# Two moves in a graph-attention kernel: the second batch's channel means ahead of the last query products of the first, and the last batch's first pair normalised a few steps later

## Chip, cores and metric

The kernel runs on one core of a Trainium2 chip. The core has five engines with a queue of instructions each: TensorE (PE; its weight loads are listed as PEld), VectorE (DVE), ScalarE (ACT), GpSimd (POOL) and SyncE (SP), which here issues the DMAs. The metric is the time of one execution in microseconds, as the median over several. Before the change it is 2466.79 us over 8 runs (2463.55 to 2468.76).

## Reference, cut to what matters

Two layers over `x` (16 batches of 1024 rows with 256 channels), both with the 1024x1024 matrix `adj`:

```python
def layer0(x, A):                      # graph convolution, batch norms
    A_norm = A + eye(n)
    deg = sum(A_norm, axis=0) + sum(A_norm, axis=1) - diagonal(A_norm)
    A_hat = A_norm * rsqrt(deg)[:, None] * rsqrt(deg)[None, :]
    agg = einsum('nm,bmd->bnd', A_hat, x)
    h = relu(batchnorm(agg @ W1.T + b1))
    return batchnorm(h @ W2.T + b2)

def layer1(x, para, adj, kv_w):        # gated graph, attention of 4 heads
    fea = transpose(x, (0, 2, 1))
    c_adj = mean(fea, axis=1)          # channel mean of each row
    diff = c_adj[:, None, :] - c_adj[:, :, None]
    A = abs(abs(sigmoid(diff) - 0.5) - 0.5) * 2.0
    Wg = adj * (A + transpose(A)) * 0.5
    q = relu(einsum('bcn,bnm->bcm', fea, Wg) * para)
    k, v = x @ kv_w
    return softmax(q k^T * scale) v    # per head

x = layernorm(x + layer0(x, adj))
x = layernorm(x + layer1(x, para, adj, kv_w))
```

All in fp32.

## The kernel before

The program orders its instructions itself: each engine's queue is filled in the order in which the Python code issues them, and no scheduler moves them. Waits follow from data and from buffers.

Layer 0 fills the first third of the time. Layer 1 runs over the 16 batches. A batch has 16 *steps*; a step `g` takes two blocks of 128 keys, one pair of heads and half of the queries. `scores(g)` (L787, tile `s`) makes the products of keys and queries into PSUM, `exps(g)` (L799, ScalarE) the exponentials `e`, `sums(g)` (L805, L808, VectorE) adds them up into `acc`, and `attend(g)` (L823, PE) multiplies them with the values into `o`. The tiles `s` have two buffers, which one step fills: the scores of step g+1 wait for the exponentials of step g. At the end of a pair of heads, `attend` copies one half of `o` on ScalarE (L834) and adds the other on VectorE (L835), as `ot`. `dens` (L852, tile `pd`) sums `acc` over the keys by PE once both pairs are done.

Around the steps lies the work for other batches, in pieces that are put into slots: 8 slots for each batch, two for each turn of the main loop, which covers four steps. A turn issues the pieces of its two slots first (sorted by `arrange`), then, for each of its steps k, the scores and exponentials of k+1 and the sums and products of k. A dictionary `between` holds pieces that are issued behind step k instead.

The pieces that matter here:

- `ln1_b` (L646, ScalarE) ends the first layer norm, and accumulates each row's sum in `cs`.
- `means` (L679, L681, VectorE) scales `cs` to the channel means and makes half of them (`hcs`).
- `crow` makes one row of 1024 means, the same on every partition. For batch 0 it does that on PE (L692). For the others it transposes `cs` on PE (L696, tile `pc`), copies 8x128 numbers on ScalarE (L698), writes them to DRAM (L699) and reads them back broadcast to 128 partitions (L700). The tile `crow` has one buffer.
- `gate`: `wg_a` makes a gate tile on ScalarE from `crow` and `hcs` or `cs` (L710, or L712 and L713), `wg_b` finishes it on VectorE with `adj` (L719, L720) and loads the next `adj` tile. Batch 1's gates belong to the first steps of batch 0's attention.
- `keys` (L736, tile `pk`, copied on ScalarE in L739), `values` (L747, tile `pv`, copied in L754), `graph` and `queries` (L769, L770).
- `x1_t` (L675, L676) transposes the normed rows on PE and copies them on VectorE, tile `px`.
- `finish_a` joins a pair of row blocks of the output and takes their moments on VectorE, with `rs` and `nm` on GpSimd (L66, L68, L914); `finish_b` normalises the pair on ScalarE (L922, two instructions) and stores it (L925). `back` (tile `pf`) and `recips` (tile `pr`, L868) serve the last half batch.

Before the first step stands an opening: eight turns of `opening`, in which batch 0's gate products (`graph0`, L1098) are accumulated over k = 0 to 7 and batch 1's rows are prepared by the lists in `second_rows`. With the last product the four query tiles are made on VectorE, out of the PSUM buffers that the first scores then take. `means(1)` follows the pieces of k = 7, and `crow(1)` is put into `between[-1]`, behind the scores and exponentials of step 0.

In the last batch (`b == B - 1`) the slots t_a and t_b of `finish_a` and `finish_b` for the first half of the queries (`hf = 0`) are worked out by the branch `elif not by_pe(b, hf)`: for the first pair (k = 0) slots 4 and 6, for the second 6 and 9. So `finish_b(15, 0)` is issued ahead of step 252's turn, in front of the exponentials of step 253.

Of the kernel before, what the change touches and what calls it, by code (L numbers as in the profile page):

```python
# [22 lines left out]
def gnn_norm_attention_kernel(  # L23
# [17 lines left out]
    B, N, C = x.shape  # L41
# [529 lines left out]
    def fast():  # L571
      with ExitStack() as fx:
# [105 lines left out]
        def means(b):  # L678
            nc.vector.tensor_scalar_mul(css[b], css[b], 1.0 / C)  # L679
            hcs[b] = sm.tile([P, NT], F32, tag="hcs", bufs=2, name=f"hcs_{b}")  # L680
            nc.vector.tensor_scalar_mul(hcs[b], css[b], 0.5)  # L681
# [130 lines left out]
        def by_pe(b, hf):  # L812
            return b == B - 1 and hf == NH - 1
# [143 lines left out]
        NC = NS // 2  # L957
        NK = NT // 2
        at, between = {}, {}

        def put(w, t, f, *a):
            at.setdefault(w * NC + t, []).append((f, a))
# [4 lines left out]
        for b in range(B):  # L967

            for hf in range(NH):
                t = (hf + 1) * (NC // NH)  # L970
                put(b, t, dens, b, hf)
                if by_pe(b, hf):
                    put(b, t, recips, b, hf)
                for k in range(KB // 2):
                    j = hf * (KB // 2) + k

                    if b * NH + hf < B * NH - 3:
                        t_f, t_a, t_b = (t + 1, t + 2 + k, t + 6 + k) if hf == 0 else (t + 1, t + 4 + k, t + 6 + k)
                    elif not by_pe(b, hf):

                        t_f, t_a, t_b = t, t + 2 * k, t + 2 + 2 * k if b < B - 1 else (t + 2, NC + 1)[k]
                    else:
                        t_f, t_a, t_b = t, t + 1 + k, t + 2 + k
                    put(b, t_f, back if by_pe(b, hf) else fetch_o, b, j)
                    if t_a == t:
                        between[(b * NC + t) * 2 + NK // 2] = [(finish_a, (b, j))]
                    else:
                        put(b, t_a, finish_a, b, j)
                    put(b, t_b, finish_b, b, j)
            if b == 0:  # L990
                continue

            if b > 1:
                put(b - 2, 2, begin, b)
                for j in range(NT // 2):
                    put(b - 2, j, load, b, j)
                    put(b - 2, j + 1, bn2_q, b, j)
                    put(b - 2, j + 2, rows, b, j)
                    put(b - 2, j + 2, ln1_a, b, j)
                    put(b - 2, j + 3, ln1_b, b, j)  # L1000
                    put(b - 2, j + 3, put_x1, b, j)
                    put(b - 2, 5 + j // 2 * 2, get_x1, b, j)
                    put(b - 2, min(6 + j, NC), x1_v, b, j)
                put(b - 2, NC - 2, means, b)
                put(b - 2, NC - 1, crow, b)

            i = 0
            for t, n in enumerate(WG):
                for i in range(i, i + n):
                    put(b - 1, t, gate, b, i)  # L1010
                i += 1
            kv = [(keys, (b, c, h)) for h in range(NH) for c in range(CT)]
            kv += [(values, (b, j)) for j in range(0, NT, 2)]
            for t, n in enumerate(KV):
                for _ in range(n):
                    f, a = kv.pop(0)
                    put(b - 1, t, f, *a)
            m = 0
            for t, n in enumerate(QG):
                for m in range(m, m + n):  # L1020
                    put(b - 1, NC - len(QG) + t, graph, b, m)
                m += 1
# [64 lines left out]
        def gate0(i):  # L1087
            wg_a(0, i)
            wg_b(0, i)
# [3 lines left out]
        def graph0(k):  # L1093
            if k == 0:
                PG0.extend(ps_s.tile([P, 2, FB], F32, tag="s", name=f"pg0_{h}") for h in range(NH))
            for h in range(NH):
                for c in range(CT):
                    nc.tensor.matmul(  # L1098
                        PG0[h][:, c, :],
                        x1s[0, k // 2][:, k % 2, ts(c, P)],  # L1100
                        wgs[0, k][:, ts(h, FB)],
                        start=(k == 0),
                        stop=(k == NT - 1),
                    )
            if k == NT - 1:
                for h in range(NH):
                    for c in range(CT):
                        queries(0, c, h, PG0[h][:, c, :])
# [27 lines left out]
        for c in range(CT):  # L1136
# [18 lines left out]
            3: [(rows, 2), (ln1_a, 2), (ln1_b, 1)],  # L1155
            4: [(x1_t, 0), (rows, 3), (ln1_a, 3)],
            5: [(ln1_b, 2), (x1_t, 1)],
            6: [(ln1_b, 3), (x1_t, 2)],
            7: [(x1_t, 3)],
        }  # L1160

        def opening(s):

            k = s + NC
            if 0 <= k < NC:
                for i in range(3 + 2 * k, min(5 + 2 * k, NT)):
                    gate0(i)
                graph0(k)
                for f, j in second_rows[k]:
                    f(1, j)  # L1170
                if k == NC - 1:
                    means(1)
                    between[-1] = [(crow, (1,))]

        for t in range(-NC // 2, max(max(at) // 2, nsteps // NK - 1) + 1):
            g = NK * t
            now = [p for s in (2 * t, 2 * t + 1) for p in [(opening, (s,))] + arrange(at.get(s, []))]
            behind = max((k + 1 for k, fa in enumerate(now) if is_short(fa)), default=0)  # L1180
            for k in range(len(now) + 1):
                if k == behind and 0 <= g < nsteps:
                    sums(g)
                if k < len(now):
                    f, a = now[k]
                    f(*a)
            for k in range(g, g + NK):
                if 0 <= k + 1 < nsteps:
                    scores(k + 1)
                    exps(k + 1)  # L1190
                if 0 <= k < nsteps:
                    if k > g:
                        sums(k)
                    attend(k)
                for f, a in between.pop(k, ()):
                    f(*a)
# [6 lines left out]
        )  # L1203

    flag = fast()


# [155 lines left out]
```

## Time and profile before

| what | value |
|---|---|
| median of 8 runs | 2466.79 us (2463.55 to 2468.76) |
| the profiled execution: time | 2468.01 us |
| the profiled execution: span from first to last instruction | 2466.2 us |
| mean granted clock of TensorE | 0.992 |
| ScalarE's exponentials (L799): 512, each | 1020 ns |
| VectorE's sums of exponentials (L808): 384, each | 1329 ns |
| ScalarE's first gates (L710): 80, each (median) | 1152 ns |
| ScalarE's normalising (L646): 128, each | 594 ns |

Lines of the order of time show: start and duration in us, engine, line, operation, output and inputs, shape, how many were merged, and in brackets how long the engine sat idle before and what ended that. Lines of waits show: engine and line that waited, for whom, total us, times, the longest. The granted clock is the share of full speed that TensorE's clock was let through at. The chain of waits from the last instruction back is no help here: the page follows it no further than the last normalisation (L922), so the places are read from the order of time.

### The profile page before, as it was taken

The page shows a single profiled execution, that of the slowest core. Times are in us where ns is not written, and L with a number is a line of the kernel's source. Part 1 is how long each engine was busy: PE and PEld are TensorE (multiplying, and loading weights), DVE is VectorE, ACT ScalarE, POOL GpSimd, SP SyncE. Part 2 cuts the span into 40 slices and gives each one's busy share as a digit, 9 for nine tenths or more (in the row PEclk, how much of TensorE's full clock was granted, in tenths as well). Part 3 has the DMA queues.
Part 4 walks back from the last instruction along what each step waited for, and adds up shares of the span by engine and source line. Part 5 has one row for each costly group of instructions (what it writes and reads, how often), then busy time and mean ns, then how long its engine had stood idle before and what let it go on. Part 6 is the DMA issues. An engine that isn't in the chain of part 4 may idle for free. (4 is left out here: it accounts for less than half of the span.)

```text
span 2466.2 us, 33875 instructions
## 1 busy us (share of the span) xinstructions
PE 2415.9 (98%) x12217; PEld 1009.8 (41%) x12217; DVE 1812.4 (73%) x2583; ACT 1094.5 (44%) x1549; POOL 777.2 (32%) x826
## 2 busy tenths in 40 slices
PE   8999999999999899999999999999999999999997
PEld 4444444444444433443434434344343343443432
DVE  5545545555776767888788888888888888888676
ACT  2000000002554455664655646656566565564644
POOL 2222232321556421314223233232332322414012
PEclk9999999999999899999999999999999999999998
DMA  3122122222677543545545545545354454554221
GB/s 137 68 86 103 71 85 101 94 77 85 213 268 265 133 120 73 149 110 121 144 101 133 140 97 146 122 118 145 82 151 114 118 148 95 139 127 109 68 44 50
DMA packets 583951, 292.73 MB, mean 119 GB/s; under 512 B 407528, under 2 KB 556512, under 8 KB 576608
## 3 DMA queue, kind: packets, MB, share of 16 engines
q1 hardware_dynamic: 583776, 290.49, 43.1%
q8 instruction: 98, 1.61, 0.3%
q14 instruction: 77, 0.63, 0.1%
HBM read 194.46 MB, written 95.94 MB: 118 GB/s over the span
## 5 line engine op out<-in xcount | busy, mean ns | idle before, releaser
L799 ACT ACTIVATE e<-s 128x1024 f32<-128x1024 f32 x512 | 496.1, 1020 | 332.1 <-PE s L787 270.6
L808 DVE TENSOR_TENSOR acc<-acc,e 128x1024 f32<-128x1024 f32 x384 | 510.2, 1329 | 115.3 <-ACT e L799 88.9
L787 PE MATMUL s<-qT,kT 64*64 64x512 f32 x4096 | 493.8, 597 | 10.9 <-ACT e L799 8.3
L823 PE MATMUL o<-e,v 64*64 64x512 f32 x4096 | 487.0, 590 | 0.0
L761 PE MATMUL pg<-wg,x 128*128 128x512 f32 x960 | 426.5, 597 | 0.0
L614 POOL TENSOR_TENSOR yt<-yt,stq 128x512 f32<-128x512 f32 x120 | 182.2, 1519 | 414.4 <-DMA yt<-yT 252.0
L761 PEld LDWEIGHTS pg<-wg,x 128*128 128x128 f32 x960 | 178.7, 190 | 238.6 <-issue 237.8
L823 PEld LDWEIGHTS o<-e,v 64*64 64x64 f32 x4096 | 157.3, 134 | 285.4 <-issue 277.7
L787 PEld LDWEIGHTS s<-qT,kT 64*64 64x64 f32 x4096 | 147.6, 133 | 306.3 <-issue 254.0
L107 ACT COPY u<-pa 128x512 f32<-128x512 f32 x15 | 8.8, 586 | 475.3 <-PE pa L312 475.3
L66 POOL TENSOR_SCALAR rs_z<-mv_z 128x2 f32<-128x2 f32 x64 | 18.2, 285 | 474.6 <-DVE mv_z L563 453.7
L720 DVE SCALAR_TENSOR_TENSOR wg<-wg,adj 128x1024 f32<-128x1024 f32 x128 | 162.8, 1303 | 2.8
L312 PE MATMUL pa<-AhT,x 128*128 128x512 f32 x360 | 161.8, 592 | 0.0
L646 ACT ACTIVATE x<-x,nm_a,rs_a 128x256 f32<-128x256 f32 x128 | 75.9, 594 | 171.9 <-POOL nm_a L636 171.5
L835 DVE TENSOR_TENSOR ot<-o,ot 128x512 f32<-128x512 f32 x64 | 44.3, 692 | 130.8 <-ACT ot L834 130.8
L747 PE MATMUL pv<-kvw,x1T 128*128 128x256 f32 x512 | 118.7, 385 | 1.3 <-ACT kT L739 1.3
L736 PE MATMUL pk<-x1T,kvw 128*128 128x512 f32 x256 | 117.8, 604 | 0.0
L66 POOL TENSOR_SCALAR rs_a<-mv_a 128x2 f32<-128x2 f32 x64 | 38.0, 593 | 237.8 <-DVE mv_a L563 236.6
L343 PE MATMUL ph<-agg,SW 128*128 128x512 f32 x240 | 112.8, 592 | 0.0
L747 PEld LDWEIGHTS pv<-kvw,x1T 128*128 128x128 f32 x512 | 96.9, 192 | 33.4 <-issue 16.0
L312 PE MATMUL pa<-T,sx 128*128 128x512 f32 x240 | 107.9, 592 | 0.0
L312 PEld LDWEIGHTS pa<-AhT,x 128*128 128x128 f32 x360 | 68.4, 190 | 86.1 <-issue 86.1
(193 smaller groups left out, 3148.7 us busy)
## 6 DMA issues: line engine op xcount, KB each, us to landing
adj<-in_adj_dram SPq DMA_DIRECT2D x128, 512.0 KB
h<-hT SPq DMA_DIRECT2D x28, 1024.0 KB
hL<-h SPq DMA_DIRECT2D x28, 1024.0 KB
ob<-o SPq DMA_DIRECT2D x248, 72.0 KB
x<-in_x_dram SPq DMA_DIRECT2D x16, 1024.0 KB
yT<-y SPq DMA_DIRECT2D x64, 256.0 KB
out_dram<-r SPq DMA_DIRECT2D x64, 256.0 KB
xr<-in_x_dram SPq DMA_DIRECT2D x62, 256.0 KB
```

The costliest lines, as they stand in the source:

```text
L312: nc.tensor.matmul(p, xs[n][:, k, :], bs[n][:, k, :], start=(k == 0), stop=(k == KN - 1))
L343: nc.tensor.matmul(p, ws[n][:, ts(f, P)], bs[n], start=True, stop=True)
L614: nc.gpsimd.tensor_tensor(y, y, sc, op)
L646: nc.scalar.activation(r, r, AF.Identity, bias=nm[:, a : a + 1], scale=rs[:, a : a + 1], accum_out=css[b][:, i : i + 1])
L720: nc.vector.scalar_tensor_tensor(t, t, 1.0, adjs[b * NT + i], op0=OP.add, op1=OP.mult)
L736: nc.tensor.matmul(p, kvw[:, k, ts(c, P)], x1Ts[b][:, k, ts(h, FB)], start=(k == 0), stop=(k == CT - 1))
L747: nc.tensor.matmul(p[:, ts(a, C)], x1Ts[b][:, k, ts(j + a, P)], kvw[:, k, C:], start=(k == 0), stop=(k == CT - 1),)
L761: nc.tensor.matmul(pg[b], x1s[b, k // 2][:, k % 2, ts(c, P)], wgs[b, k][:, ts(h, FB)], start=(k == 0), stop=(k == NT - 1))
L787: nc.tensor.matmul(t[r * HD : (r + 1) * HD, h, :], kTs[b, pair][h * HD : (h + 1) * HD, ts(2 * cb + r, HD)], qTs[b, pair, hf][h * HD : (h + ...
L799: nc.scalar.activation(E[g, a], S.pop((g, a)), AF.Exp)
L808: nc.vector.tensor_add(ACC[b, hf, pair], ACC[b, hf, pair], E[g, a])
L823: nc.tensor.matmul(O[b, hf, pair][r][h * HD : (h + 1) * HD, :], vs[b][r * HD : (r + 1) * HD, cb, pair * P + h * HD : pair * P + (h + 1) * HD],
```

## The change

Two edits, in the lists that set the order.

In the opening, `means(1)` and `crow(1)` are issued with k = 6: the means behind `ln1_b(1, 3)`, the row behind the transposes of the third pair, so ahead of the products of k = 7, batch 0's queries and the first scores. `second_rows` takes None for a piece that has no pair.

In the last batch, `finish_b(15, 0)` leaves slot 6 and goes into `between`, behind step 254, so behind the exponentials of steps 253, 254 and 255.

```diff
@@ -979,6 +979,9 @@
                         t_f, t_a, t_b = t, t + 2 * k, t + 2 + 2 * k if b < B - 1 else (t + 2, NC + 1)[k]
+                        if b == B - 1 and k == 0:
+                            between[(b * NC + t_b) * 2 + NK // 2] = [(finish_b, (b, j))]
+                            t_b = None
                     else:
                         t_f, t_a, t_b = t, t + 1 + k, t + 2 + k
@@ -986,7 +989,8 @@
                     else:
                         put(b, t_a, finish_a, b, j)
-                    put(b, t_b, finish_b, b, j)
+                    if t_b is not None:
+                        put(b, t_b, finish_b, b, j)
@@ -1155,7 +1159,7 @@
-            6: [(ln1_b, 3), (x1_t, 2)],
+            6: [(ln1_b, 3), (means, None), (x1_t, 2), (crow, None)],
             7: [(x1_t, 3)],
@@ -1167,10 +1171,7 @@
                 for f, j in second_rows[k]:
-                    f(1, j)
-                if k == NC - 1:
-                    means(1)
-                    between[-1] = [(crow, (1,))]
+                    f(1) if j is None else f(1, j)
```

The lines behind the edits move by one (L1098 of before is L1102 after); the number of instructions stays.

## The prediction

> **What bounds the kernel now.** I read the page's busy shares first, then TensorE's waits over the span, then the order of time around each place that the change touches, and the granted clock there.
>
> ```profile
> span 2466.2 us, 33875 instructions
> PE 2415.9 (98%) x12217; PEld 1009.8 (41%) x12217; DVE 1812.4 (73%) x2583; ACT 1094.5 (44%) x1549; POOL 777.2 (32%) x826
> ...
> PE s L787 <- ACT e L799: 8.3, 3, 3.5
> ...
> PE pv L747 <- ACT kT L739: 1.3, 1, 1.3
> ```
>
> TensorE (PE) is busy for 98% of the span, so a change gains only where PE waits. Attention's score products (`s`) wait for ScalarE's exponentials (`e`) three times, 8.3 us in all. Two of the three lie where the change works: 3.13 us in the opening of the attention, 3.46 us in the last batch.
>
> The opening, in order of time (start, duration, engine, line; idle before it and its releaser in brackets):
>
> ```profile
> 866.11 0.69 DVE L676 COPY x1T<-px 128x512 f32<-128x512 f32 x1 [3.18 <-PE px L675]
> ...
> 872.98 0.27 PE L696 MATMUL pc<-ident,cs 128*8 128x128 f32 x1
> 873.09 7.03 PE L736 MATMUL pk<-x1T,kvw 128*128 128x512 f32 x16
> 873.83 0.24 ACT L698 COPY crow<-pc 8x128 f32<-8x128 f32 x1
> 874.09 0.35 SPq L699 DMA_DIRECT2D crow_d<-crow  x1
> 875.32 0.34 SPq L700 DMA_DIRECT2D crow<-crow_d  x1
> 879.74 1.15 ACT L710 ACTIVATE wg<-crow,hcs 128x1024 f32<-128x1024 f32 x1 [5.67 <-DMA crow<-crow_d]
> 881.41 1.99 PE L747 MATMUL pv<-kvw,x1T 128*128 128x256 f32 x8 [1.29 <-ACT kT L739]
> 889.49 1.92 ACT L799 ACTIVATE e<-s 128x1024 f32<-128x1024 f32 x2
> 890.55 3.36 PE L787 MATMUL s<-qT,kT 64*64 64x512 f32 x16 [3.13 <-ACT e L799]
> 895.73 1.90 PE L787 MATMUL s<-qT,kT 64*64 64x512 f32 x16
> ```
>
> The row of channel means (`crow`) goes out through DRAM and back: 874.07 (copy's end) to 879.74, 5.67 us. ScalarE sits in front of its first gate activation until then. Its queue then holds 9.75 us of gates and copies (879.74 to 889.49) ahead of the exponentials that PE needs. PE pays 1.29 us before `pv`, and 3.13 us before `s`.
>
> The last batch, and the granted clock there (in the last two lines the columns are stretch, length, busy time of PE, PEld, DVE, ACT and POOL with counts, then the clock):
>
> ```profile
> 2433.25 1.90 PE L823 MATMUL o<-e,v 64*64 64x512 f32 x16
> 2436.56 1.09 ACT L922 ACTIVATE r<-r,nm,rs_z 128x256 f32<-128x256 f32 x2 [4.22 <-POOL nm L914]
> 2438.61 3.69 PE L787 MATMUL s<-qT,kT 64*64 64x512 f32 x16 [3.46 <-ACT e L799]
> 2439.97 5.21 DVE L808 TENSOR_TENSOR acc<-acc,e 128x1024 f32<-128x1024 f32 x4
> 2450.01 1.07 PE L852 MATMUL pd<-acc,ones 128*32 128x512 f32 x8
> 2452.94 0.26 DVE L868 RECIPROCAL RD<-pr 128x16 f32<-128x16 f32 x1 [1.51 <-PE pr L866]
> ...
> 891.00:892.00 1.00, 1.00 (x11) 0.23 (x7) 1.00 (x1) 0.41 (x1) 0.97 (x1) 0.50 0.98 348
> 2440.00:2441.00 1.00, 1.00 (x8) 0.25 (x4) 1.00 (x2) 0.34 (x1) 0.79 (x1) 0.50 0.00 0
> ```
>
> ScalarE waits 4.22 us for GpSimd's `nm` with the exponentials queued behind. After both long waits of PE the granted clock is 0.50: `s` takes 3.36 and 3.69 us for 16 where other rows have 1.90. From stretch to stretch the clock is low from about 890.9 to 894.4 and from 2437.2 to 2444.0.
>
> **Part 1, the means earlier.** Moved: two VectorE scalings (L679, L681; 0.16 and 0.17 us), one PE transpose, one ScalarE copy (0.24 us), two DMAs. As built, VectorE does the scalings ahead of the L676 copy at 866.11. Their input, ScalarE's last row sum, ends at 864.38, and VectorE is idle for 3.18 us there: cost nothing; without that idle time, 0.33 us on the way to the queries. The copy behind the scalings would wait if the sums came late.
>
> PE does the transpose after the third `px` group, at about 865.9. Its input is then over 1 us old. It takes 0.11 us of PE (872.98 to 873.09), taken back at 872.98. Its PSUM buffer and that of the last `px` group change places; both were long free. `crow` has one buffer, whose last reader of batch 0 starts at 847.59 and takes 1.1 us. SyncE's queue: the last load ahead was issued by 853.30, so nothing holds the DMAs; batch 2's first loads, behind them, go up to 7.5 us earlier too, into DMA engines with a share of 0.00 from 860 to 872. GpSimd is passed by nothing.
>
> So the copy starts at about 866.3, ends at 866.55, and with the same 5.67 us the row is back at 872.2. ScalarE gets free only after its second exponential, 1.02 us from 872.91+0.11 = 873.02, at 874.05. The row is 1.8 us early, and the gates start at 874.05 instead of 879.74.
>
> From there I step both queues forward with the durations of before. `pk` runs 872.95 to 879.85 without a wait for `kT`; ScalarE now waits a little for `pk`. `pv` to 881.7; `s` to 883.45; `o` to 885.2. ScalarE: the fourth `kT` copy from 879.98, a gate from 880.5, `v` from 881.87 (it needs `pv`), two activations to 884.5, first exponential to 885.5. PE waits 0.3 us for it instead of 3.13 us, too little to lower the clock by any row here. `s` then begins at 885.55, loses 0.1 us on the second exponential, `o` from 887.4, and the `s` of 895.73 comes at 889.1: **6.6 us**. Bounds: 7.1 us if ScalarE never held PE (`s`, `o`, `s`, `o` from 881.7 end at 888.6, at the 1.72 us from start to start that undisturbed groups show), 5.0 us where the clock had stayed full in the kernel before (5.18 us from 890.55 to 895.73 would have been about 3.5). I take 6.6, the stepping through this profile. Between 895.73 and 2400 PE waits nowhere for ScalarE or a DMA, so the shift stays to the end.
>
> **Part 2, the first finished pair later.** Two ScalarE activations (1.09 us) and a store move behind the last exponentials. No other DMA is passed on SyncE's queue, nothing on GpSimd's. In times of before, the exponential after L834's copy starts at 2432.6, its two parts end by 2434.6, and PE goes from `o` (2433.25) straight on: `s` 2434.97, `o` 2436.7, `s` 2438.4, two `o` groups to 2443.55. Before they ended at about 2450.0. The moved activations run from 2441.4 to 2442.5, ahead of the last L834 copy at 2443.6, so they are hidden; without that gap they would cost up to 1.09 us.
>
> But VectorE doesn't move. From 2428.47, where it gets `ob` by DMA, it works without a gap until 2439.97, and the six sums L808 follow, 7.8 us by the six at 2407.19 (7.87), to 2447.8. `pd`, the sums over keys, needs them. Before, they ended at 2449.53 and PE's `o` set the time. At full clock: half of `pd` from 2447.93, eight `pf` transposes (0.117 us apart) after `ot` at 2448.5, four `pr`, reciprocal at 2450.1: 2.8 us before 2452.94. But PE then has stood for 3.8 to 4.3 us, longer than both waits after which the clock was 0.50. At half clock `pd` takes 1.0 instead of 0.5, `pf` 1.9 instead of 0.94, `pr` 1.1 instead of 0.6: reciprocal at 2451.9, **1.1 us** gained. I take this end, the nearest rows being the 3.13 and 3.46 us waits; 2.8 stays as a bound, and 0 below, where the kernel before had kept its clock (then its `o` would have ended at 2447.3, with VectorE in charge).
>
> The Trainium skill, page "TensorE: Matmul & The Clock Gate", section "What's actually happening", says that the clock is halved after an idle window of about 3.4 us, and that the windows run freely and don't start with the work. It speaks against part 2, which makes a longer gap than it closes. The stretches agree: 890.9 to 894.4 is one such window, 2437.2 to 2444.0 two. By it a gap of 3.8 us that falls across two windows could leave the clock full, and part 2 would give 2.8 us; by the rows alone it gives 1.1 us.
>
> **The sum.** 6.6 + 1.1 = 7.7 us. The profiled execution took 2468.01 us, 1.8 us beyond its span; 2460.3 after the change. It is 1.2 us above the median of 2466.79, so I predict 2459.1 us.
>
> **Rivals.**
> 1. The tail keeps its clock: 6.6 + 2.8 = 9.4 us, 2457.4. For it: half of `pd` can run before the gap. Against: both gaps of this size here were followed by 0.50.
> 2. The kernel before mostly pays less for its clock than the profile shows: 5.0 + 0, 2461.8. For it: the profiled execution is above the median by 1.2 us. Against: 1.2 us is less than the 2.7 us that it would take.
> 3. The row comes back late, and ScalarE's wait stays in part. At 3 us later than 874.05 part 1 gives 3.6 us, 2462.1 with part 2; at 5.7 us later nothing, 2465.7. Against: idle DMA engines, 1.8 us to spare. This is also where the change would not do what it says.
> 4. Slower: the transpose now stands in PE's queue ahead of the last query products. If the last row sum were late, PE would stand there. GpSimd feeds it, and its three steps took 0.22, 0.71 and 0.50 us; in other rows the same take 1.02, 1.74 and 4.58. With the slow ones the scalings end at about 870.6, PE stands 4.7 us and runs up to two low stretches (3.4 us lost). That eats 8.1 of 7.7: 2467.2, and more with later sums. It begins from sums 1.2 us late and passes the gain from about 5.5 us. Against: VectorE's work beside GpSimd there is the same as before.
>
> **How the numbers follow.** Forecast 0.62, rival 1 0.13, rival 2 0.12, rival 3 0.10, rival 4 0.03. The range 2456.0 to 2463.5 takes rivals 1, 2 and most of 3, with about 1.3 us for the spread of the median (single runs lie within 2463.55 to 2468.76). 0.2% is 4.9 us, about what a measurement of this kernel can tell from no change: under 2461.9 is faster. Forecast, rival 1 and half of rival 2 lie there: 0.81. Slower by as much needs more than rival 4's price: 0.02. The rest, 0.17, is the same.
>
> **What would show it.** Right: `pc` ahead of the last query products, the gates from about 874 with no DMA wait, no wait of 1 us of PE from 873 to 890, clock 1.00 there; in the last batch no wait of ScalarE for `nm` before the exponentials, no wait of `s`, instead `pd` waiting some 4 us for VectorE's `acc`, at clock 0.50. Wrong: a wait for `crow`, a wait of PE for `cs` near 866, or the 6.6 us given back before 2400.

## Result, and the profile after

| | median us | runs |
|---|---|---|
| before | 2466.68 | 32 |
| changed | 2460.16 (2458.43 to 2462.45) | 12 |

The ratio is 0.9974, with a 95% interval of 0.9966 to 0.9981: 6.5 us less, where 7.7 us were forecast (2459.1; the range was 2456.0 to 2463.5). The profiled execution of the changed kernel took 2460.43 us, 7.6 us less than the profiled one of before.

TensorE is busy for 2412.5 us of a span of 2458.7, 98% as before. Two lines from the list of its waits in the changed kernel (engine and line that waited, for whom, total us, times, longest):

```profile
PE pd L852 <- DVE acc L808: 2.7, 1, 2.7
...
PE s L787 <- ACT e L799: 1.7, 1, 1.7
```

Of the three waits of the scores for the exponentials (8.3 us) only the one of 1.7 us that the change doesn't touch is left. A longer one is new: `pd`, the sums over keys, waits for VectorE.

The opening of the changed kernel, in order of time (PE, ScalarE, SyncE put together by start):

```profile
866.04 0.60 PE L675 MATMUL px<-ident,x 128*128 128x128 f32 x4
866.47 0.27 PE L696 MATMUL pc<-ident,cs 128*8 128x128 f32 x1
866.78 0.25 ACT L698 COPY crow<-pc 8x128 f32<-8x128 f32 x1 [1.83 <-PE pc L696]
868.29 0.34 SPq L700 DMA_DIRECT2D crow<-crow_d  x1
874.51 1.14 ACT L710 ACTIVATE wg<-crow,hcs 128x1024 f32<-128x1024 f32 x1
886.03 2.00 PE L787 MATMUL s<-qT,kT 64*64 64x512 f32 x16
889.57 1.90 PE L787 MATMUL s<-qT,kT 64*64 64x512 f32 x16
```

The gates (L710) begin at 874.51 straight behind the second exponential, with no bracket: nobody waits for the row any more. The scores of 886.03 have no bracket either; before they sat idle for 3.13 us. To compare executions I count from the third `px` group, since layer 0 ended 0.57 us later in this one (866.04 against 865.47): to the scores of 889.57 it takes 23.53 us, where before it took 30.26 us (865.47 to 895.73). The opening gave 6.73 us. This counts a stretch at half clock that the profile of before had in its opening (890.9 to 894.4) and this one has not; it is worth some 1.7 us (5.18 us from 890.55 to 895.73, where two undisturbed groups take 3.44).

The last batch of the changed kernel, in order of time, and then one stretch of its granted clock (stretch, length, busy time and count of PE, PEld, DVE, ACT, POOL, clock, DMA share, GB/s):

```profile
2427.02 1.90 PE L823 MATMUL o<-e,v 64*64 64x512 f32 x16
2428.73 1.90 PE L787 MATMUL s<-qT,kT 64*64 64x512 f32 x16
...
2433.26 7.87 DVE L808 TENSOR_TENSOR acc<-acc,e 128x1024 f32<-128x1024 f32 x6
2437.43 1.05 PE L852 MATMUL pd<-acc,ones 128*32 128x512 f32 x4
2441.18 1.80 PE L852 MATMUL pd<-acc,ones 128*32 128x512 f32 x4 [2.70 <-DVE acc L808]
2444.67 0.65 PE L866 MATMUL pr<-ident,dt 128*128 128x128 f32 x4
```

```profile
2442.00:2443.00 1.00, 1.00 (x5) 0.09 (x2) 0.00 (x0) 0.00 (x0) 0.00 (x0) 0.50 0.00 0
```

The scores run on behind `o` without a gap. VectorE's six sums take 7.87 us without a gap, and the second half of `pd` waits for them; behind that gap the clock is 0.50. I measure this tail from the products of step 252 (here 2427.02) to the first `pr` (2444.67): 17.65 us, against 19.05 us before (2433.25 to 2452.30). So in these two executions the tail gave 1.40 us and the opening 6.73.

### The profile page after: what moved, and what is told of

It is laid out like the page before. It is cut to its first block, busy times and chain, and to the rows that moved or that the text cites. A ratio compares the mean times of both kernels' runs of the same rounds, so it can differ in the third digit from the quotient of the medians.

```text
span 2458.7 us, 33873 instructions
## 1 busy us (share of the span) xinstructions
PE 2412.5 (98%) x12217; PEld 1008.4 (41%) x12217; DVE 1810.3 (74%) x2583; ACT 1094.0 (44%) x1549; POOL 774.9 (32%) x826
## 5 line engine op out<-in xcount | busy, mean ns | idle before, releaser
L747 PEld LDWEIGHTS pv<-kvw,x1T 128*128 128x128 f32 x512 | 97.1, 192 | 31.7 <-issue 16.2
```

Of the source, the lines that this page charges most:

```text
L747: nc.tensor.matmul(p[:, ts(a, C)], x1Ts[b][:, k, ts(j + a, P)], kvw[:, k, C:], start=(k == 0), stop=(k == CT - 1),)
```

## Experiments

All are compared with the kernel before on the same chip and in the same rounds. The kernel before took 2465.89 us beside e1 to e4, 2466.09 beside e5 to e8 and 2467.24 beside e9 to e11, so runs of different groups are compared by their ratios. Lengths of the tail (from step 252's products to the first `pr`) come from each run's one profiled execution.

| run | what | median us | ratio to before (95%) | tail us | clock in the tail |
|---|---|---|---|---|---|
| before | | 2466.68 | | 19.05 | 0.50 from 2437.2 to 2444.0 |
| changed | both edits | 2460.16 | 0.9974 (0.9966 to 0.9981) | 17.65 | 0.50 from 2441.3 |
| e1 | both, again | 2460.76 | 0.9976 (0.9966 to 0.9986) | 17.83 | 0.50 |
| e11 | both, third time | 2459.81 | 0.9970 (0.9960 to 0.9981) | 17.62 | 0.50 |
| e2 | first edit alone | 2458.62 | 0.9972 (0.9963 to 0.9982) | 16.21 | 1.00 |
| e10 | first edit alone, again | 2457.66 | 0.9966 (0.9952 to 0.9979) | 16.03 | 1.00 |
| e3 | second edit alone | 2466.42 | 1.0004 (0.9995 to 1.0013) | 17.14 | 1.00, then 0.50 from 2448.7 |
| e4 | row 4 us later | 2459.32 | 0.9977 (0.9968 to 0.9987) | 16.32 | 1.00 |
| e5 | tail filled, 7 rounds | 2459.97 | 0.9976 (0.9966 to 0.9986) | 17.47 | 1.00 |
| e9 | tail filled, 4 rounds | 2459.05 | 0.9968 (0.9956 to 0.9980) | 16.27 | 1.00 |
| e6 | both, last sums on PE | 2456.26 | 0.9959 (0.9946 to 0.9973) | 14.05 | 1.00 |
| e7 | first alone, last sums on PE | 2459.48 | 0.9976 (0.9967 to 0.9985) | 17.65 | 1.00 |
| e8 | e6 and queries reordered | 2455.34 | 0.9957 (0.9943 to 0.9970) | 14.05 | 1.00 |

### The changed kernel again, and each edit alone

> The changed kernel once more, beside the three below. By my steps: about 2460 us, 6 to 8 us under the kernel before; in the trace the first step-2 scores without a wait of 1 us, the row of means long back when the gates begin, and in the tail a PE wait of 3 to 4 us for the sums with the granted clock at 0.50 behind it. If the clock in the tail depends on where the idle stretch falls, another execution may show 1.00 there and an end 1 to 1.7 us earlier.

> Only the first edit (means and row earlier); the last batch as before. Theory: 6.6 us under the kernel before, the opening as in the changed kernel, and in the last batch the old wait of 3.5 us of the scores for the exponentials. Rival, the kernel before mostly keeps its clock in the opening: 5.0 us. Rival, the parts are not additive and the last batch brings most: under 3 us.

> Only the second edit (the first pair normalised behind the last exponentials); the opening as before. Theory: PE's scores run on without the 3.5 us wait, but VectorE's six sums end at the same place, and the tail runs at half clock: 1.1 to 1.4 us under the kernel before, too little for the times to show alone. Rival, the tail keeps its clock: 2.8 us. Rival, the wait only moves: 0.

The edits are those of the change: e2 leaves out

```diff
-                        if b == B - 1 and k == 0:
-                            between[(b * NC + t_b) * 2 + NK // 2] = [(finish_b, (b, j))]
-                            t_b = None
```

and e3 puts `means(1)` and `crow(1)` back behind k = 7. The first edit alone is 0.9972 of before, the second alone 1.0004, where 1.1 to 1.4 us of gain were expected. So by the ratios the gain is the first edit's. (The interval of e3 reaches from 1.2 us of gain to 3.2 us of loss; 1.1 us is at its edge, and not ruled out by this time alone.) In e2's opening, third `px` group to the scores in question takes 864.34 to 887.88, 23.54 us, as in the changed kernel. In e3 it takes 29.87 us (866.38 to 896.25), against 30.26 before, again with the clock at 0.50 behind the wait of the scores (892.2 to 895.6).

Why the second edit brings nothing shows in the tail of e2 (first edit alone, the first pair normalised in its old place), PE and VectorE in order of time, with a stretch of its clock:

```profile
2425.41 1.90 PE L823 MATMUL o<-e,v 64*64 64x512 f32 x16
2430.44 2.00 PE L787 MATMUL s<-qT,kT 64*64 64x512 f32 x16 [3.13 <-ACT e L799]
2431.79 7.86 DVE L808 TENSOR_TENSOR acc<-acc,e 128x1024 f32<-128x1024 f32 x6
2439.24 1.52 PE L852 MATMUL pd<-acc,ones 128*32 128x512 f32 x8
2441.62 0.60 PE L866 MATMUL pr<-ident,dt 128*128 128x128 f32 x4
```

```profile
2431.00:2432.00 1.00, 1.00 (x16) 0.36 (x12) 0.86 (x5) 0.70 (x2) 0.00 (x0) 1.00 0.16 53
```

The old wait of 3.13 us is there, but the clock stays at 1.00 behind it: `s` takes 2.00 us where the profile before had 3.69. `pr` comes 16.21 us after step 252's products. With both edits and a full clock (e4 below) it is 16.32. At equal clock the second edit is worth nothing: PE's wait goes, but VectorE's six sums end 14.24 us after step 252's products start in e2, 14.11 in the changed kernel and 14.35 in e4, with the edit or without it.

### The row's way

> The changed kernel with the row's transpose behind the products of k = 7 and the last px group, still ahead of the first scores: it starts 4 us later. Theory, the row's arrival sets ScalarE's gates: copy at about 870.9, row back 5.7 us later at 876.8 instead of long before 874.5; the gates begin 2.3 us later, PE waits about 1.8 us for the exponentials of step 1 and the kernel loses 1.6 us against the changed one (2461.8). Rival, what counts is only that the transpose no longer stands behind the first scores: no loss, 2460.2.

```diff
-            6: [(ln1_b, 3), (means, None), (x1_t, 2), (crow, None)],
-            7: [(x1_t, 3)],
+            6: [(ln1_b, 3), (means, None), (x1_t, 2)],
+            7: [(x1_t, 3), (crow, None)],
```

The opening and the tail of e4, in order of time:

```profile
869.62 0.26 ACT L698 COPY crow<-pc 8x128 f32<-8x128 f32 x1 [5.70 <-PE pc L696]
875.35 1.15 ACT L710 ACTIVATE wg<-crow,hcs 128x1024 f32<-128x1024 f32 x1 [1.88 <-DMA crow<-crow_d]
886.17 2.01 PE L787 MATMUL s<-qT,kT 64*64 64x512 f32 x16 [1.41 <-ACT e L799]
...
2441.62 1.05 PE L852 MATMUL pd<-acc,ones 128*32 128x512 f32 x4 [2.94 <-DVE acc L808]
2443.54 0.60 PE L866 MATMUL pr<-ident,dt 128*128 128x128 f32 x4
```

Where the row comes later, ScalarE waits 1.88 us for its DMA, and PE 1.41 us for the exponentials, where I expected 2.3 and 1.8. From the row's copy to the gates it takes 5.47 us (869.88 to 875.35). The opening is 24.71 us, 1.18 us longer than in the changed kernel. So the row's arrival is what sets the gates. The time doesn't show this: 2459.32, not the 2461.8 expected. In the profiled execution the tail kept its clock, which is worth 1.3 to 1.5 us (16.32 against 17.65 and 17.83), and the third `px` group, ahead of the row in both, came 1.04 us earlier than in the changed kernel's profile (865.00 against 866.04). Together that is more than the loss. Why the median of all ten runs is low isn't shown, as only one of them has a trace.

### The tail's clock

> The changed kernel, in whose last half batch PE makes pair 0's sums over keys seven times instead of once (the same result, some 3 us of PE) while it stands for VectorE's sums of pair 1. Theory, the half clock of the tail comes from that standing alone: clock 1.00 through pd, pf and pr, and from the start of the products of step 252 to the first pr 16.3 us (as where the clock stayed full) instead of 17.65 and 17.83; 1.4 us under the changed kernel where that one is slow, nothing where it isn't. Rival, VectorE alone sets the tail: no difference. Rival, products of 32 columns don't keep the clock up: 0.50 again.

> The filler with four rounds of pair 0's sums instead of seven: seven took 0.79 us each and ended 2 us too late, four end just ahead of VectorE's acc. Theory: clock 1.00 through the tail, 16.3 us from step 252's products to the first pr, 1.4 us less than the changed kernel shows at half clock (17.65, 17.83). Rival, the tail's clock costs nothing on the path: 17.5 again.

```diff
-                for h in range(2):
+                for _ in range(4 if by_pe(b, hf) and pair == 0 else 1):
+                    for h in range(2):
```

(7 in place of 4 in e5.) The tail of e9, with the same stretch of the clock as above:

```profile
2437.34 3.63 PE L853 MATMUL pd<-acc,ones 128*32 128x512 f32 x16
2441.29 1.05 PE L853 MATMUL pd<-acc,ones 128*32 128x512 f32 x4 [0.33 <-DVE acc L808]
2443.20 0.60 PE L867 MATMUL pr<-ident,dt 128*128 128x128 f32 x4
```

```profile
2442.00:2443.00 1.00, 1.00 (x9) 0.73 (x8) 0.00 (x0) 0.61 (x2) 0.00 (x0) 1.00 0.00 0
```

With PE busy in the gap, the clock stays at 1.00 and the tail is 16.27 us, 1.4 us shorter than at half clock. VectorE's sums end where they did (14.31 us after step 252's products start), so the 1.4 us is the price of the clock alone. That the filling kept the clock up is likely but not shown: e4 kept it in its profile without any. e5 filled the gap too long (32 of these products took 6.20 us; some 3 us had been expected for the added ones) and lost the gain again. Over the times e9 is 0.8 us under e11 beside it, which six and eight runs can't tell from nothing.

### VectorE relieved, with and without the second edit

> The changed kernel with the last step's two sums of exponentials (2.6 us of VectorE) taken over by PE: the products with ones read these two tiles directly, ahead of acc. Theory, VectorE's sums hold the tail: acc is ready 2.6 us earlier, PE goes on with 1 us of products in the gap, the clock stays 1.00, and from step 252's products to the first pr it takes 13.4 to 13.9 us instead of 16.3 (full clock) or 17.7 (half): some 3 to 4 us under the changed kernel, about 2456.5. Rival, VectorE isn't what holds it: as before or 0.5 us later through the added products.

> The same relief of VectorE, with the first edit alone (the first pair normalised in its old place). Theory, the second edit brings nothing only because VectorE holds the tail: with VectorE relieved the scores' wait of 3.1 to 3.5 us for the exponentials is on the path, 16.2 to 16.9 us from step 252's products to the first pr at full clock (over 18 at half), so 3 us or more behind e6. Rival, the second edit is worthless in any case: the same time as e6.

```diff
+            if g >= nsteps - 1:
+                LATE.extend(E[g, a] for a in range(2))
+                return
...
-                    nc.tensor.matmul(p[k : k + 32, :], ones32, acc[:, h, :], start=True, stop=True)
+                parts = (LATE if by_pe(b, hf) and pair == NP - 1 else []) + [acc]
+                for n, t in enumerate(parts):
...
+                            p[k : k + 32, :], ones32, t[:, h, :], start=(n == 0), stop=(n == len(parts) - 1)
```

The tail of e6 (both edits), then of e7 (first edit alone):

```profile
2426.44 1.90 PE L828 MATMUL o<-e,v 64*64 64x512 f32 x16
2432.46 5.20 DVE L813 TENSOR_TENSOR acc<-acc,e 128x1024 f32<-128x1024 f32 x4
2437.32 1.46 PE L859 MATMUL pd<-e,ones 128*32 128x512 f32 x6
2440.49 0.60 PE L875 MATMUL pr<-ident,dt 128*128 128x128 f32 x4
```

```profile
2427.43 1.90 PE L828 MATMUL o<-e,v 64*64 64x512 f32 x16
2432.64 2.00 PE L787 MATMUL s<-qT,kT 64*64 64x512 f32 x16 [3.31 <-ACT e L799]
2445.08 0.60 PE L875 MATMUL pr<-ident,dt 128*128 128x128 f32 x4
```

In e6 four sums are left to VectorE (5.20 us), PE sums the last step's tiles itself, nothing of `pd` waits, and the tail is 14.05 us: 2.3 us less than the 16.32 of a full clock, 3.6 less than the changed kernel's own profile. In e7 the old wait of 3.31 us is on the path again, and the tail is 17.65 us at full clock, 3.6 us behind e6 (3.2 us by the medians). So with VectorE relieved the second edit is worth 3.6 us. Not all of that is gained on the first edit alone: in e7 the relief itself makes the tail 1.44 us longer than e2's 16.21, because the eight added products stand in PE's way (from the start of `pd` to the start of `pf` it takes 2.72 us in e7, 1.45 in e2). For e7's tail 16.2 to 16.9 us had been expected. Against e2, the relief and the second edit together give 2.16 us at full clock.

> e6, and batch 0's four query tiles with all multiplications that read the PSUM buffers ahead of the last three cut-offs, so that the second half of the first scores gets its buffer earlier. Theory: the wait of 0.79 us for VectorE goes, ScalarE's gates start 0.8 us earlier (the row was back by then), and the time falls by 0.8 us against e6. Rival, the row or pk then holds ScalarE: no gain.

In e8 the three multiplications of L769 that follow the first query tile stand ahead of the remaining cut-offs of L770. The first scores of e8:

```profile
869.84 2.10 PE L787 MATMUL s<-qT,kT 64*64 64x512 f32 x16
```

The two halves run as one, without the wait of 0.79 us for VectorE. The opening takes 22.67 us (865.33 to 888.00), 0.86 us less. At 2455.34 us, ratio 0.9957, it has the lowest median here, 10.6 us under before by the ratio, from five runs.

### Both edits against the first alone

> The first edit alone once more, beside the changed kernel on the same chip. Theory, at full clock the second edit is worth nothing (16.2 against 16.3 us in the tail), and what differs is how often the half clock meets the scores' wait of one (2.8 us) or the pd wait of the other (1.4 us): the medians within 2 us, the first edit alone spread over two groups some 2.5 us apart. Rival, the second edit is worth the 1.1 us that I put down for it: the first edit alone is 1.1 us slower.

> The changed kernel beside the two above: about 2460 us; level with the first edit alone or up to 2 us behind it by the theory, 1.1 us ahead of it by the rival.

Beside each other twice, the first edit alone had the lower median: 2458.62 against 2460.76, 2457.66 against 2459.81. Eight of its 15 runs lie from 2457.1 to 2457.9, seven from 2459.1 to 2462.1; the changed kernel's 29 runs lie from 2458.4 to 2462.5. That is not the 1.1 us of gain that I had put down. Whether the second edit costs something, as the medians say, is not settled: the intervals of the ratios overlap.

The two groups are not explained by the tail's clock, as I had expected. The profiled executions of e2 (2457.53 us) and e10 (2459.10 us), of the same kernel, lie one in each group, and both kept the clock in the tail. They differ earlier: layer 0's last product (L494) starts at 808.3 and at 810.2, and the third `px` group, first of e2 and then of e10, lies 1.86 us apart. The last four lines are e10's wait in the last batch and the waits at `pd` of e1, e3 and e11:

```profile
864.34 0.60 PE L675 MATMUL px<-ident,x 128*128 128x128 f32 x4
866.20 0.60 PE L675 MATMUL px<-ident,x 128*128 128x128 f32 x4
...
2432.13 2.00 PE L787 MATMUL s<-qT,kT 64*64 64x512 f32 x16 [2.94 <-ACT e L799]
2441.57 1.83 PE L852 MATMUL pd<-acc,ones 128*32 128x512 f32 x4 [2.85 <-DVE acc L808]
2447.91 1.25 PE L852 MATMUL pd<-acc,ones 128*32 128x512 f32 x4 [2.75 <-DVE acc L808]
2440.76 1.92 PE L852 MATMUL pd<-acc,ones 128*32 128x512 f32 x4 [2.67 <-DVE acc L808]
```

Over all profiles here this group comes at 864.3 to 866.4. So what lies ahead of both edits moves an execution by up to 2 us, about as much as these medians differ.

## Why the prediction was right, point by point

- **The opening, 6.6 us: right, and for the reasons given.** 6.73 us by the two profiles (6.34 against the opening of e3). The gates were forecast at 874.05 and came at 874.51, in an execution that was 0.57 us late as it came there; the second scores were forecast to wait 0.3 us, and run 0.3 us late (886.03 against 884.01 + 1.72). e4 shows that the row's arrival is the cause. The 6.6 us, like the 6.73, hold the half clock of the opening before; it was there in both profiles with the old opening (before and e3), and how many other executions have it isn't known.
- **The shift stays to the end: right.** From the scores of the opening (889.57) to step 252's products (2427.02) it takes 1537.45 us, before 1537.52 (895.73 to 2433.25).
- **The last batch: the mechanism right, the term mis-sized.** VectorE's six sums ended the tail, the new wait stood at `pd`, and the clock fell to 0.50 behind it, all as forecast, and by the two profiles it gave 1.40 us where I had 1.1. The gap was too long in the prediction: 3.8 to 4.3 us there, 2.70 measured, since the sums ended 14.11 us after step 252's products start, not 14.55, and the first half of `pd` filled 1.05 us of the gap, where 0.5 was reckoned: half of `pd` takes as long as the whole, 1.07 us. So "a longer gap than it closes" was wrong too: the one that it closes was 3.46 us. But I set a tail at half clock against another at half clock, because the profile of before had one. e2 and e10 show the same old wait (3.13 and 2.94 us) with the clock at 1.00, and then the tail takes 16.2 and 16.0 us. Behind the waits at `pd` (2.67 to 2.85 us) the clock fell in time to slow the tail in four executions, and not in e4, behind 2.94 us. So the step that failed is "I take this end, the nearest rows being the 3.13 and 3.46 us waits": a pair of rows that both fell on one side. Over many executions the term is nearer to 0, the lower bound named there, than to 1.1: alone it measured a ratio of 1.0004, and with the first edit both medians are higher than without it.
- **Rivals 1 and 2** were each half of this: a tail that keeps its clock (e4), and a kernel before that pays less than its profile shows. The second is concluded from the tails of e2 and e10; the kernel before was profiled once, at half clock. What was wrong was to take them for two cases instead of the spread of one kernel's executions. The sum came out 1.2 us too high, about the size of this term. That the 6.6 us alone meet the 6.5 measured so closely is in part luck: by the ratios the first edit by itself gave 6.9 and 8.4 us.
- **Rivals 3 and 4 fell.** The row was early, and the transpose stood behind sums that were ready.

That the same gap halves the clock in one execution and not in another is what the Trainium skill's page "TensorE: Matmul & The Clock Gate", section "What's actually happening", leads one to expect: it says that the windows run freely and don't begin with the work. The traces agree: with both edits the clock was 0.50 from 2441.3 to 2444.8 in one execution, and in e4, with a wait of the same kind, it fell only at 2446.7, behind the last `pr`.

## What to carry to other kernels

Before a wait is removed, look at what the other engines would have ended at: here VectorE's 7.9 us of sums ended where PE's wait of 3.1 us let PE end at full clock (e2), so taking the wait away brought nothing until VectorE was relieved too. Relieving VectorE alone (e7) brought nothing either; both together gave 2.2 us at full clock (e6 against e2). A time that a half-speed clock has stretched belongs to one execution: cost a change at both clocks, against before at both clocks, and not against the one state that the profile happened to show. A small result that goes out to DRAM and back (5.5 to 5.7 us here for 4 KB out and a broadcast in) is worth issuing as soon as its inputs exist, ahead of long work that needs nothing from it.

## What the runs showed of the hardware that was not expected

A wait of PE of about 3 us halved the clock in some executions and left it at 1.00 in others of the same or a like kernel: 3.46 us with 0.50 before, 3.31 us in e7 and 3.13 us in e2 with 1.00, 2.70 us with 0.50 in the changed kernel. Where it fell within the path, it cost 2.8 us before (19.05 against 16.2 in e2) and 1.4 us after (17.65 against 16.3 in e4 and e9). And products for different groups of 32 rows of the same output ran side by side: eight of the sums over keys, on four groups of `pd`, took 1.07 us before, and four on two groups took no less, 1.05 us, in the changed kernel. Repeated on the same two groups they add up: 16 took 3.63 us in e9, and 32, 28 of them on two groups, 6.20 us in e5.
